# Attention on selected tokens: turning gathered rows by transposing DMA instead of on TensorE

## The chip, the cores and the metric

The kernel runs on one core of one Trainium2 chip. The metric is device time in microseconds (us) of one execution, from the slowest (here the only) core; less is better.

TensorE is called PE below (PEld is its weight load), VectorE DVE, ScalarE ACT, GpSimd POOL, and SyncE SP. SP computes nothing: it issues DMA transfers, in order, and waits before each until its source is ready. POOL here issues the indirect DMA transfers, which gather or scatter rows by a list of indices. Each engine runs its own instructions in order.

## The reference

Sixteen batches of x, each 512 features by 1024 tokens, get an attention layer with 8 heads of 64 features added. Query, key and value are the same projection. A token mask of zeros and ones decides which keys count, and rows of masked-out queries get uniform weights:

```python
xt = jnp.transpose(x, (0, 2, 1))
q = xt @ Wq.T
qh = q.reshape(B, T, NH, dk).transpose(0, 2, 1, 3)
scores = scale * jnp.einsum('bhqd,bhkd->bhqk', qh, qh)
logits = (scores * cmask + (1.0 - cmask) * NEG) * rmask
attn = jax.nn.softmax(logits, axis=-1)
ctx = jnp.einsum('bhqk,bhkd->bhqd', attn, qh)
out = ctx.transpose(0, 2, 1, 3).reshape(B, T, D) @ Wo.T
return x + jnp.transpose(out, (0, 2, 1))
```

## The kernel before, in words

**What is computed.** About half of the 1024 tokens of a batch are unmasked. The kernel packs them: per batch it computes on 544 columns (`C`), which hold the unmasked tokens first. A masked token's result is the projected mean of the values, so it needs only the mean of x over the tokens, kept as one more column (`CM`, column 544).

**Numbers.** Products that need float32 precision are made of float16 parts: a number a is split into a high part (a rounded to float16) and a low part (the remainder, in float16). A product takes three matmuls: high x high, low x high, high x low.

**The stages of a batch.**

- `slots` (for a group of batches) and `index` (L237 to L259, one batch) turn the mask into row numbers: eight small matmuls at L246 and an `idx` tile at L248; two masks of padding columns follow (L257, L259).
- `gather` (L319) posts five indirect transfers: four tiles `xa` of 128 tokens by 512 features in float32, and one tile `xt` of 32 tokens. `rows` (L310) issues them on POOL. The `xa` tiles are kept until the end of the batch's work, since the result is added to them and scattered back; they come from a ring of 13 buffers.
- `xt(b, k)` (L388) turns tile k, so that the features lie on the partitions. PE transposes it in blocks of 128 by 128 against an identity into a PSUM bank of the ring `pm` (L398; 16 large and 4 small blocks per batch). `xsplit` (L351) then splits the bank: ACT writes the high part into `xh` (L358), DVE the low part into `xl` (L359). After the fifth tile the mean column is added (L408, L355, L356).
- `query` (L411) multiplies `xh` and `xl` with the split weights, 12 matmuls for each of 8 combinations of a block of 128 features and a half of the columns (L421); ACT takes the result out of PSUM (L424). `qsplit` (L429) splits q on DVE, and four transfers on SP copy the parts into the tile `xx` (L442 to L445).
- `value` and `value_tail` transpose q for the values; `top` (L499) takes the largest squared length of q per head on DVE and turns it on PE (L509), and `bottom` (L513) makes the softmax shift of it.
- `scores` (L542) multiplies `xx` with itself (L580); ACT takes the exponential (L584). `attend` (L589) multiplies with the values (L597, L600).
- `recip_sums` and `recip_rows` (L608 to L642) take the inverse of the row sums. PE turns them (L633), DVE copies them out of PSUM (L636), SP writes them to DRAM (`rd<-rr`, L638) and reads them back spread over 64 partitions (`rb<-rd`, L641). `norm` (L645) multiplies with them on DVE (L664) and splits the result.
- `project` (L687) multiplies with the output weights (L680), DVE adds the result to the gathered tile (L685), POOL scatters it (L764). Masked tokens are gathered, added to and scattered by `late` and `rest` (L695 to L757).

**What sets the order.** `run` (L800 on) works on three batches at a time. While the scores of batch b go step by step (18 steps), a list `m` of other work is spread over the steps by the estimated cost of each entry: the last part of batch b-1 (its norm and projections), and the preparation of batch n = b+1 (`xt`, `query`, `value`). The list of a usual batch begins

```python
m = xt(n)[:1] + early[0] + xt(n)[1:2] + chunk2 + xt(n)[2:3] + early[1] + xt(n)[3:] + tp + query(n, 0, 0) + query(n, 0, 1) + bt + value(n, 0)
```

and the index and the gathers of batch b+2 come after the middle of it. A gather, a scatter or a `late` gather is not issued when it is posted: `issue` sends one transfer per step, and `once(dma, self.beat)` makes it wait for the latest matmul recorded at that time, so that POOL's transfers keep pace with PE. `later` puts a transfer of SP off to the next step. The tile framework then orders the instructions of each engine and sets the semaphores; `high_priority` moves an entry forward.

**Rings.** `pm` has two PSUM banks, which all small products share in turn: a bank is free again when its reader on ACT or DVE is done. The scores have two banks of their own (`pss`), so that PE can be two score tiles ahead of the exponentials.

Of the kernel before, what the change touches and what calls it, by code (L numbers as in the profile page):

```python
# [19 lines left out]
P = 128  # L20
# [14 lines left out]
CM = C  # L35
HG = H // 2
# [13 lines left out]
class Fast:  # L50
# [78 lines left out]
    def setup2(self):  # L129
# [4 lines left out]
        self.xh = fixed("xh", [P, DC, CQ], F16)  # L134
        self.xl = fixed("xl", [P, DC, CQ], F16)
        for t in (self.xh, self.xl):
            nc.gpsimd.memset(t[:, :, CM + 1:], 0.0)

# [10 lines left out]
    def load(self, name, c, half=None, after=None):  # L149
# [4 lines left out]
        raw = self.sb([P, D], F32, "xa", 13)[:, cols]  # L154
# [167 lines left out]
    def gather_now(self, b, j):  # L322
        s = self.st[b]
        if j < 4:
            s["xa"].append(self.rows(s["idx"][:, j:j + 1], self.sb([P, D], F32, "xa", 13)))
        else:
            s["xt"] = self.rows(s["idx"][:CT, 4:5], self.sb([P, D], F32, "xt"))
# [23 lines left out]
    def xsplit(self, dst, src, scaled=False):  # L351
        nc = self.nc
        with self.tc.high_priority(offset=HPO):
            if scaled:
                nc.vector.tensor_copy(self.xh[dst], src)  # L355
                self.xs = nc.vector.tensor_tensor(self.xl[dst], src, self.xh[dst], ALU.subtract).ins  # L356
            else:
                nc.scalar.activation(self.xh[dst], src, AF.Copy, scale=SX)  # L358
                self.xs = nc.vector.scalar_tensor_tensor(self.xl[dst], src, SX, self.xh[dst], ALU.mult, ALU.subtract).ins  # L359

    def range_x(self, b, c):
# [4 lines left out]
        nc.vector.tensor_reduce(s["top4"][:, c:c + 1], self.xh[:, c, :CM + 1], AX.X, ALU.max, apply_absolute_value=True)  # L366
# [21 lines left out]
    def xt(self, b, k):  # L388
# [3 lines left out]
        x = s["xa"][k] if k < 4 else s["xt"]  # L392
        if b == 0:
# [6 lines left out]
        self.xsplit((slice(None), slice(None), slice(k * P, k * P + n)), pt)  # L400
        self.last_xs = self.xs
        if k == 4:
            ms = self.sb([P, DC], F32, "ms", 2)
            m = s["ms2"].rearrange("p (c h) -> p c h", h=2)
            if b < 2:
                with self.behind(s["at"]):
                    nc.vector.tensor_tensor(ms, m[:, :, 0], m[:, :, 1], ALU.add)
            nc.vector.tensor_scalar(ms, ms if b < 2 else s["ms2"][:, :DC], SX / T, None, ALU.mult)  # L408
            self.xsplit((slice(None), slice(None), CM), ms, True)

    def query(self, b, e, g):  # L411
# [7 lines left out]
        for c in range(DC):  # L419
            for w, xx in ((wh, self.xh), (wh, self.xl), (wl, self.xh)):  # L420
# [74 lines left out]
    def shift(self, b, g):  # L495
# [639 lines left out]
```

## Time and profile before

| What | Value |
|---|---|
| Three timed runs | 1137.52, 1138.30, 1139.32 us; median 1138.3 |
| The profiled execution | 1133.56 us; span from its first to its last instruction 1131.8 us |
| Instructions | 23296 |
| Granted TensorE clock, mean | 0.992 of full speed |
| DMA | 181.35 MB in 78122 packets, mean 160 GB/s |
| HBM | 92.34 MB read, 33.91 MB written |

How to read the profile: the page gives the busy time of each engine as a share of the span, then the same in 40 equal slices of it, one digit per slice in tenths (9 is 90% or more). Then come the DMA queues with packets, MB and the share that their packets took of the time of 16 DMA engines (q1 is that of SP's transfers, q0 that of POOL's indirect ones). The chain is the work that ended last, followed back from the last instruction to what released each step. In a row of costs, the line number is that of the kernel, `out<-in` names the tiles, then come the partitions x elements of each and the number of instructions; behind the first bar stand the busy time in us and the mean length of one in ns, behind the second the idle time of that engine just before them, with what ended most of it. Matmuls overlap, so the length of one is more than its share of the busy time.

### The profile page before, as it was taken

The numbers are of one execution on the slowest core, as the hardware profiler recorded it, in microseconds if no ns is written. First come the engines' busy times: TensorE is split into PE (matmuls) and PEld (weight loads), VectorE is DVE, ScalarE is ACT, GpSimd is POOL, SyncE is SP. The second block draws the span as 40 slices with busy tenths as digits, with TensorE's granted clock in tenths as the row PEclk, the third lists the DMA queues.
The fourth block names the chain that finished last, engine by engine and source line by source line (L and its number), as shares of the span: only waits on it lengthen the run. The fifth ranks groups of instructions, "written<-read, shape, count | busy, mean of one in ns | idle before, by whom it ended". The sixth has DMA issues, their size and how long they took to land.

```text
span 1131.8 us, 23296 instructions
## 1 busy us (share of the span) xinstructions
PE 1090.5 (96%) x8386; PEld 707.9 (63%) x8386; DVE 731.6 (65%) x2369; ACT 676.2 (60%) x1716; POOL 289.1 (26%) x303
## 2 busy tenths in 40 slices
PE   7899999999999999999999999999999999998997
PEld 6566666666666666566666666566666666665543
DVE  6687567675665767667665666856576675655643
ACT  5776666666566666566565665666656566654540
POOL 3101021322202222222222232222222232214642
PEclk9899999999999999999999999999999999999999
DMA  6745554656546454655655566455655654545652
GB/s 212 218 117 151 143 159 128 191 142 179 149 127 175 124 201 137 171 175 158 189 150 165 154 177 185 129 181 144 195 166 156 188 152 130 149 126 174 204 161 77
DMA packets 78122, 181.35 MB, mean 160 GB/s; under 512 B 15008, under 2 KB 16800, under 8 KB 78000
## 3 DMA queue, kind: packets, MB, share of 16 engines
q1 hardware_dynamic: 56816, 111.62, 35.6%
q0 software_dynamic: 21184, 68.18, 18.7%
q8 instruction: 68, 1.11, 0.4%
q14 instruction: 54, 0.44, 0.1%
HBM read 92.34 MB, written 33.91 MB: 112 GB/s over the span
## 4 chain that ended last, share of the span: by engine, by line
PE 66%; DVE 14%; DMA 11%; issue 5%; ACT 2%; POOL 1%; SPq 1%; DVEq 0%; POOLq 0%; ACTq 0%
PE pav L597 19%; PE pss L580 16%; PE pm L680 13%; PE pm L421 8%; DMA rb<-rd 4%; PE pm L398 2%; DMA rd<-rr 2%; PE pav L600 2%; DMA xi<-x_in,idx 2%; PE pm L467 1%; DVE c L664 1%; DMA xx<-hl 1%; PE pm L633 1%; DVE tmp L458 1%; PE pss L555 1%
## 5 line engine op out<-in xcount | busy, mean ns | idle before, releaser
L584 ACT ACTIVATE p<-pss,nm 128x544 f32<-128x544 f32 x512 | 363.3, 714 | 231.5 <-PE pss L580 219.5
L580 PE MATMUL pss<-xx 128*128 128x272 f16 x2048 | 303.0, 281 | 4.2 <-DMA xx<-hl 2.7
L597 PE MATMUL pav<-p,v 128*64 128x272 f32 x2048 | 297.5, 402 | 0.9 <-ACT c L604 0.9
L580 PEld LDWEIGHTS <-xx 128*128 128x128 f16 x2048 | 192.1, 99 | 85.4 <-issue 41.2
L597 PEld LDWEIGHTS pav<-p,v 128*64 128x64 f32 x2048 | 140.6, 137 | 105.4 <-issue 40.9
L764 POOL DMA_INDIRECT y_out<-xa,idx x68 | 70.9, 1043 | 302.4 <-PE pss L580 163.6
L421 PE MATMUL pm<-xh,wqh 128*128 128x274 f16 (+1 forms) x512 | 143.9, 281 | 0.1
L421 PE MATMUL pm<-xl,wqh 128*128 128x274 f16 (+1 forms) x512 | 143.2, 280 | 0.2 <-DVE xl L359 0.2
L421 PE MATMUL pm<-xh,wql 128*128 128x274 f16 (+1 forms) x512 | 143.3, 280 | 0.0
L313 POOL DMA_INDIRECT xa<-x_in,idx x68 | 70.0, 1029 | 184.6 <-PE pss L580 89.3
L421 PEld LDWEIGHTS <-wqh 128*128 128x128 f16 x1024 | 99.9, 99 | 21.9 <-issue 3.4
L584 ACT ACTIVATION_READ_ACCUMULATOR p<-pss,nm 128x1 f32 x512 | 102.7, 201 | 0.0
L685 DVE SCALAR_TENSOR_TENSOR xa<-pm,xa 128x512 f32<-128x512 f32 x60 | 41.4, 689 | 89.6 <-PE pm L680 89.5
L313 POOL DMA_INDIRECT xi<-x_in,idx x60 | 59.6, 994 | 153.9 <-PE pss L555 53.9
L680 PE MATMUL pm<-woh,ch 128*128 128x512 f16 x240 | 91.0, 379 | 0.3 <-DVE ch L667 0.3
L680 PE MATMUL pm<-woh,cl 128*128 128x512 f16 x240 | 91.1, 379 | 0.1
L680 PE MATMUL pm<-wol,ch 128*128 128x512 f16 x240 | 91.0, 379 | 0.0
L424 ACT ACTIVATE q<-pm 128x272 f32<-128x272 f32 (+1 forms) x128 | 51.0, 398 | 64.0 <-PE pm L421 63.8
L764 POOL DMA_INDIRECT y_out<-xi,idx x60 | 60.9, 1015 | 92.0 <-PE pss L580 72.9
L664 DVE TENSOR_TENSOR c<-c,rb 128x544 f32<-128x544 f32 x64 | 46.2, 722 | 49.2 <-DMA rb<-rd 42.5
L680 PEld LDWEIGHTS <-ch 128*128 128x128 f16 x480 | 46.1, 98 | 41.0 <-DVE ch L667 0.8
L751 DVE TENSOR_TENSOR xi<-xi,ub 128x512 f32<-128x512 f32 (+1 forms) x60 | 40.1, 687 | 40.2 <-DMA xi<-x_in,idx 27.7
(191 smaller groups left out, 1585.5 us busy)
## 6 DMA issues: line engine op xcount, KB each, us to landing
xx<-hl SPq DMA_DIRECT2D x256, 136.0 KB
xm<-x_nat_in SPq DMA_DIRECT2D x56, 512.0 KB
rb<-rd SPq DMA_DIRECT2D x128, 136.0 KB
pt<-c SPq DMA_DIRECT2D x64, 136.0 KB
pt<-p SPq DMA_DIRECT2D x64, 136.0 KB
ub<-ud SPq DMA_DIRECT2D x16, 256.0 KB
xi<-x_nat_in SPq DMA_DIRECT2D x8, 256.0 KB
xa<-x_in,idx POOLq DMA_INDIRECT x68, 4.3
```

Of the source, the lines that this page charges most:

```text
L313: dma = self.nc.gpsimd.indirect_dma_start(out=tile[:n], out_offset=None, in_=self.x, in_offset=bass.IndirectOffsetOnAxis(ap=idx, axis=0))
L398: self.pe = nc.tensor.transpose(pt[:, c, :], x[:n, c * P:(c + 1) * P], self.ident[:n, :n]).ins
L421: self.beat = nc.tensor.matmul(pq, lhsT=w[:, c, e * P:(e + 1) * P], rhs=xx[:, c, cols], start=(k == 0), stop=(k == 3 * DC - 1)).ins
L424: nc.scalar.activation(s["q"][:, e, cols], pq, AF.Copy, scale=1.0 / (SX * SW))
L580: self.beat = nc.tensor.matmul(pt[:, g, :CH], lhsT=xx[:, 2 * k, i * P:(i + 1) * P], rhs=xx[:, 2 * k + a, g * CH:(g + 1) * CH], start=(a == ...
L584: self.exp = [nc.scalar.activation(t.rearrange("p (g c) -> p g c", g=2), pt[:, :, :CH], AF.Exp, bias=s["nm"][p // HG][:, p % HG:p % HG + 1 ...
L597: nc.tensor.matmul(s["pav"][k * DK:(k + 1) * DK, g, :CH], lhsT=s["v"][p][:, i, k * DK:(k + 1) * DK], rhs=ps[k][:, cols], start=(i == 0), s ...
L664: nc.vector.tensor_tensor(c, c, s["rb"][p], ALU.mult)
L680: nc.tensor.matmul(po[:cols.stop - cols.start], lhsT=a[:, e, cols], rhs=w[:, e, :], start=(e == 0 and k == 0), stop=(e == DC - 1 and k == 2))
L685: self.nc.vector.scalar_tensor_tensor(x, po, 1.0 / (SX * SW), x, ALU.mult, ALU.add)
L751: self.nc.vector.tensor_tensor(x[:n], x[:n], s["ub"][:n], ALU.add)
L764: dma = self.nc.gpsimd.indirect_dma_start(out=self.out, out_offset=bass.IndirectOffsetOnAxis(ap=idx, axis=0), in_=x, in_offset=None)
```

## The change

The transposes of batches 2 to 15 no longer run on PE. Batches 0 and 1 go as before. For the others, a new function `turn` splits a gathered tile where it lies, tokens on the partitions, into a float16 tile `hx` with the high and the low part side by side (128 x 1024). A transposing DMA transfer on SP then writes it, turned, into the tile `xhl`, which holds high and low part of all 8 blocks of features and has two buffers, since batch b+2 is now turned while batch b+1 is still read. Its rows are 560 wide (`CX`) instead of 546. The mean column is written twice (columns 544 and 545) in place of a mean and a zero.

The order moves too. The index of b+2 comes behind the first two queries of batch n instead of at the end of the list's middle part; its gathers are posted right after it; the five `turn` entries stand among the queries and values of the second half. `top` is cut in two: its DVE part (`peaks`) comes sooner than its transpose. The ring `xa` grows from 13 to 15 buffers, and the DMA descriptor scratch is set to 4096 bytes per partition; before, the kernel left it at its default.

```diff
+    def room(self, b):
+        s = self.st[b]
+        s["xhl"] = self.sb([P, 2 * DC, CX], F16, "xhl", 2)
+        s["xh"], s["xl"] = s["xhl"][:, :DC], s["xhl"][:, DC:]
+
+    def xsplit(self, hi, lo, src):
+        nc = self.nc
+        nc.scalar.activation(hi, src, AF.Copy, scale=SX)
+        self.xs = nc.vector.scalar_tensor_tensor(lo, src, SX, hi, ALU.mult, ALU.subtract).ins
+
+    def turn(self, b, k):
+        nc, s = self.nc, self.st[b]
+        n = P if k < 4 else CT
+        x = s["xa"][k] if k < 4 else s["xt"]
+        if "xhl" not in s:
+            self.room(b)
+        hx = self.sb([P, 2, D], F16, "hx", 2)
+        self.xsplit(hx[:n, 0], hx[:n, 1], x[:n])
+        out, src = s["xhl"][:, :, k * P:k * P + n], hx[:n].rearrange("p a d -> p (a d)")
+        self.later(lambda: nc.sync.dma_start_transpose(out=out, in_=src))
+        if k == 4:
+            self.mean(b)
...
-            s["xa"].append(self.rows(s["idx"][:, j:j + 1], self.sb([P, D], F32, "xa", 13)))
+            s["xa"].append(self.rows(s["idx"][:, j:j + 1], self.sb([P, D], F32, "xa", 15)))
...
-                m = xt(n)[:1] + early[0] + xt(n)[1:2] + chunk2 + xt(n)[2:3] + early[1] + xt(n)[3:] + tp + query(n, 0, 0) + query(n, 0, 1) + bt + value(n, 0)
-                m += query(n, 1, 0) + late + P_(0) + query(n, 1, 1) + P_(1)
+                ahead = b + 2 < B
+                index = [(0.5, L(self.index, b + 2))] if ahead else []
+                take = lambda *js: [(0, L(self.gather, b + 2, j)) for j in js] if ahead else []
+                turn = lambda k: [(0, L(self.turn, b + 2, k))] if ahead else []
+                m = early[0] + pk + (xt(n)[:3] if n == 1 else []) + chunk2 + (xt(n)[3:] if n == 1 else [])
+                m += query(n, 0, 0) + early[1] + tp + query(n, 0, 1) + bt + index + value(n, 0) + take(0, 1, 2, 4)
+                m += query(n, 1, 0) + late + P_(0) + take(3) + query(n, 1, 1) + P_(1)
                 m += [(0, L(self.range_x, n, c)) for c in range(DC)]
-                r = P_(2) + value(n, 1) + [(0.25, L(self.value_tail, n, 0))] + query(n, 2, 0) + query(n, 2, 1)
-                r += query(n, 3, 0) + [(0.1, L(self.top, n, 0))] + value(n, 2) + query(n, 3, 1)
-                r += [(0.1, L(self.bottom, n, 0))] + P_(3) + value(n, 3)
-                r += [(0.25, L(self.value_tail, n, 1)), (0, L(self.means, n))]
-                if b + 2 < B:
-                    m += [(0.5, L(self.index, b + 2))]
-                    r[1:1] = [(0, L(self.gather, b + 2, j)) for j in range(5)]
+                r = P_(2) + turn(0) + value(n, 1) + [(0.25, L(self.value_tail, n, 0))] + query(n, 2, 0)
+                r += [(0, L(self.peaks, n, 0))] + turn(1) + query(n, 2, 1)
+                r += [(0.1, L(self.top, n, 0))] + query(n, 3, 0) + turn(2) + value(n, 2) + query(n, 3, 1)
+                r += [(0.1, L(self.bottom, n, 0))] + turn(3) + P_(3) + value(n, 3)
+                r += [(0.25, L(self.value_tail, n, 1))] + turn(4) + [(0, L(self.means, n))]
...
-    nc = bacc.Bacc("TRN2", target_bir_lowering=False, num_devices=1)
+    nc = bacc.Bacc("TRN2", target_bir_lowering=False, num_devices=1, dynamic_dma_scratch_size=4096)
```

## The prediction

> **What bounds the kernel now.** I read the page's busy table and the 40 slices first, then one row for the middle of the run, then the costs by line with shapes kept apart, then the waits.
>
> ```profile
> span 1131.8 us, 23296 instructions
> PE 1090.5 (96%) x8386; PEld 707.9 (63%) x8386; DVE 731.6 (65%) x2369; ACT 676.2 (60%) x1716; POOL 289.1 (26%) x303
> PE   7899999999999999999999999999999999998997
> PEclk9899999999999999999999999999999999999999
> DMA  6745554656546454655655566455655654545652
> ...
> q1 hardware_dynamic: 56816, 111.62, 35.6%
> q0 software_dynamic: 21184, 68.18, 18.7%
> ...
> PE 66%; DVE 14%; DMA 11%; issue 5%; ACT 2%; POOL 1%; SPq 1%; DVEq 0%; POOLq 0%; ACTq 0%
> ```
>
> PE is full in all slices but the first and the last few, at full clock, and holds two thirds of the chain. The next row is the stretch from the first to the last of the steady-state transposes (us; then busy us of PE, PEld, DVE, ACT, POOL; clock, DMA share, GB/s).
>
> ```profile
> 49.30:984.40 935.10, 919.91 (x7143) 602.01 (x7144) 624.89 (x2032) 584.82 (x1480) 222.90 (x220) 1.00 0.55 159
> ```
>
> In 935 us PE idles 15.2 us, about 1.1 us in each of the 14 batches of some 67 us. DVE is at 67%, ACT at 63%, DMA at 55%. So PE bounds every batch: PE work taken out is time gained unless a new wait puts it back. The rows that go, or lie next to what is new:
>
> ```profile
> L398 PE MATMUL pm<-ident,xa 128*128 128x128 f32 x240 | 37.5, 280 | 2.1 <-DVE tmp L487 1.3 <-ACT v L469 0.5
> L398 PE MATMUL pm<-ident,xt 32*128 32x32 f32 x60 | 6.5, 227 | 0.0
> L359 DVE SCALAR_TENSOR_TENSOR xl<-pm,xh 128x512 f16<-128x512 f32 x60 | 39.9, 684 | 19.5 <-ACT xh L358 18.7
> L358 ACT ACTIVATE xh<-pm 128x512 f16<-128x512 f32 x60 | 34.8, 600 | 10.4 <-PE pm L398 9.9
> L163 DVE SCALAR_TENSOR_TENSOR wol<-xa,woh 128x512 f16<-128x512 f32 x4 | 2.7, 670 | 0.0
> L162 ACT ACTIVATE woh<-xa 128x512 f16<-128x512 f32 x4 | 2.4, 634 | 0.0
> ```
>
> 280 ns is the length of one transpose, but they are pipelined: 37.5 us over 240 is 0.156 us each, 6.5 over 60 is 0.108.
>
> **1. Transposes leave PE.** Batches 0 and 1 keep theirs; 14 batches lose 16 large and 4 small ones each: 224 x 0.156 + 56 x 0.108 = 41 us. In the PE timeline at 443 to 449 us one batch's run takes 1.02 + 0.59 + 0.50 + 0.36 = 2.47 us, times 14 = 35 us. I take **-38** (-41 to -35). The PE waits in front of them go too: 2.1 us in the first row, nothing in the second; **-2** (-4 to 0). What is late next is the exponentials and DVE's chain, costed in 3 and 4.
>
> **2. The split reads SBUF instead of PSUM.** Same number of ACT and DVE instructions. The weight split (L162, L163) does the same from SBUF: ACT 634 for 600 ns, DVE 670 for 684 ns; 56 times that is +1.9 us on ACT, -0.8 us on DVE, on engines with a third of their time free. **0**. It also moves: the copies and subtractions leave the crowded start of a batch for its second half. Into the start come the index (1.22 us of DVE at L242, 0.17 at L248) and the two pad masks (0.35 + 0.30), some 2.0 us, where 4 x 0.68 + 0.28 = 3.0 us of subtractions leave: **0**; if the cover fails, PE's eight small index matmuls (L246) wait up to 1.2 us per batch (+17).
>
> **3. A new wait on ACT.** In the changed program's order, in 12 of the 14 batches ACT's copy of the second gathered tile stands directly behind the exponential of the same scores that release that gather. Nearest rows: a gather into xa lands 2.7 / 3.7 / 8.3 us (min, median, max) after its issue. Let the scores end at 0. ACT does one or two exponentials (0.71 us each) and the first tile's copy (0.6), and is at the second copy by about 2; the rows land at 3.7; the copy ends at 4.3. Queued behind it are the next exponentials. PE has, after those scores, one projection (12 at 0.216 = 2.6 us), half an attend (1.0) and eight score matmuls (0.9); at 4.5 us it needs a score bank that an exponential from 4.3 to 5.0 frees. So PE waits 0.5 us; nothing if the rows land in 2.7; 1.8 us if they take 5.0, as the xi gather issued at 449.23 did. 12 x 0.5 = **+6** (0 to +22). The third tile's copy comes 4 us after its release, the tail's later still; the fourth's gather waits for a scatter (landing median 3.4), but ACT gets there at about the same time: 0.
>
> **4. Transposing transfers on SP's queue.** No row shows one. Each moves 256 KB; 70 are added (56 full, 14 of a quarter size), 59.5 full ones. By bytes: q1 moved 111.62 MB in 0.356 x 16 x 1131.8 us, 17.3 KB per engine-us, 277 GB/s on 16; 256 KB take 0.95 us. By packets: q1's cost 0.356 x 16 x 1131.8 / 56816 = 0.113 us each; if each 256-byte row of a 128-column block is a packet, 1024 of them on 16 engines take 7.2 us. I take 0.95, the nearest row being xx<-hl, SBUF to SBUF as well, whose 136 KB take SP 0.46 to 0.60 us to issue and land in 4.0 (493.71 us in the chain). Then DMA gains 57 us of work, 55% to 60%: harmless. What is queued behind on SP is the point. A transfer waits there for DVE's subtraction; behind it stand the four xx<-hl issues of a query, then rd<-rr, then rb<-rd, for which DVE's L664 waits already:
>
> ```profile
> L664 DVE TENSOR_TENSOR c<-c,rb 128x544 f32<-128x544 f32 x64 | 46.2, 722 | 49.2 <-DMA rb<-rd 42.5 <-SPq L1105 4.8 <-ACT p L584 1.9
> L685 DVE SCALAR_TENSOR_TENSOR xa<-pm,xa 128x512 f32<-128x512 f32 x60 | 41.4, 689 | 89.6 <-PE pm L680 89.5
> ```
>
> Behind L664 on DVE stands the next projection's L685, which frees one of the two pm banks, and the next rr copy, which frees the other. Before, rr at 468.25 led to rb at 476.73, 8.5 us, and PE hardly noticed. After, the third tile's subtraction (0.68) and its transfer (0.95) come ahead, so rb lands about 1.6 us later; PE, meeting both banks, pays about half: 14 x 0.8 = **+11** (0 to +28, if none or all of 2 us reaches PE). That queries wait for transfers I cost at nothing: tiles 0 to 3 are turned some 20 us before the query that reads them, and the first query waits for tiles 0 to 2 only. Cover lost, it is a landing, 4 us per batch.
>
> *A rule against the change.* PE's row shows 0.280 us for one block, 0.156 in a row. The Trainium skill, page "VectorE: DVE Perf Modes", section "The three transpose paths", gives 390 ns on TensorE and 1309 ns by DMA for a 128x128 block, and advises TensorE where PSUM will do as the target. Laid end to end, eight blocks would be 10.5 us per transfer (an estimate from that page), and the sum would be that of the slower rival below. The page "Advanced Engine Details and Errata", section "X-Bar Transpose (TRN2)", says that on trn2 such DMAs are as fast as regular ones, 350 to 400 GB/s, which makes 0.7 us (an estimate again) and the sum as here. No run here yet shows which.
>
> **5. The rest.** POOL issues the same gathers and scatters; those of batch b+2 go some 25 us sooner, onto a queue at 24%, and two more xa buffers (15) hold them. The smaller descriptor scratch has no row: from nothing to each of 284 indirect transfers waiting for the one before (3.7 us); POOL's instructions now take 0.9 to 1.0 us and mostly wait for PE, so **0**. Start and end keep their work: 0 (-3 to +3).
>
> **Sum:** -38 - 2 + 6 + 11 = -23 us. The profiled execution took 1133.56 us (span 1131.8 and 1.8 around it), so 1110.6 for it; the three timed runs have a median 4.7 us above that, and 1138.3 - 23 = **1115 us**.
>
> **Rivals.**
> - *The gain is kept almost whole.* For it: before, a 42.5 us wait of DVE for rb left PE at 98%; gathers may land under 3.7. Then -38 - 2 + 0 to 3: about 1099.
> - *Slower: the transfer is dear.* If one costs nearer 7.2 us than 0.95, SP is held, and the xx, rd and rb transfers of the same queue stand behind it; DMA goes to 55% + 59.5 x 7.2 / 1132 = 93%. rb then lands 7.9 us later instead of 1.6; with about 3 us taken up by slack PE waits 5 us per batch in place of 0.8: -40 + 6 + 70 = +36, some 1174. It decides from the point where PE loses 2.8 us per batch, at a transfer of about 5 us. Against it: only the count of packets speaks for it.
> - *The change does not do what it says:* transposes stay on PE or gathers are not sooner. The program's order shows 280 transposes gone and the index moved; hardly possible.
> - *A new bound:* ACT at 585 of 910 us and DVE at 625 of 910 stay under 70%. Not likely.
>
> **Chances.** Forecast (1103 to 1130): 0.46. Kept whole (under 1103): 0.23. Waits eat the gain but for a few us (1130 to 1136): 0.04; to within 0.2%, about what a measurement of this kernel can tell from no change: 0.05. Slower: 0.22, of which the dear transfer 0.14 and a sum of the upper bounds of 2, 3 and 4 (-40 + 17 + 22 + 28 = +27, 1165) 0.08. Faster is 0.46 + 0.23 + 0.04 = 0.73. The range goes from 1095, the fast end of the case kept whole, to 1145, which takes in the beginning of the slower one; outside are 0.04 below and 0.16 above.
>
> **What would show it.** Step 1: PE busy near 1050, and no L398 row after batch 1. Step 3: ACT's split copy with a wait for the xa gather of 1 to 2 us, a dozen times. Step 4: SP's transpose issues near 1 us each, and the wait of c for rb above 42.5 but PE idle under 2.5 us per batch; issues of 4 us or more, or DMA over 75%, would bring the slower case. PE waiting for an index, or for a transposed tile, would show steps 2 or 4 wrong.

## The result, and the profile after

| | Before | After |
|---|---|---|
| Median of four runs each | 1138.0 us (1137.5 to 1139.3) | 1194.4 us (1192.9 to 1199.6) |
| Profiled execution (span) | 1133.56 us (1131.8) | 1195.61 us (1193.9) |
| PE busy / idle in the span | 1090.5 / 41.3 us | 1081.8 / 112.1 us |
| Mean granted TensorE clock | 0.992 | 0.971 |

After over before is 1.050 (95% interval 1.047 to 1.053): slower, where 1115 us and a range of 1095 to 1145 had been predicted.

The page of the changed kernel, with the engines' busy time, PE and its clock in 40 slices, DMA, SP's and POOL's queues, and the chain that ended last:

```profile
span 1193.9 us, 22892 instructions
PE 1081.8 (91%) x8106; PEld 688.2 (58%) x8106; DVE 734.5 (62%) x2369; ACT 683.7 (57%) x1716; POOL 297.2 (25%) x301
PE   7899989898898999989799897998999899899997
PEclk9899999999899999999989999999999999999999
DMA  6746845757564584866648666474866648545552
...
q1 hardware_dynamic: 119984, 127.22, 42.3%
q0 software_dynamic: 21184, 68.18, 18.7%
...
PE 38%; DMA 20%; DVE 16%; issue 15%; ACT 4%; SPq 3%; POOL 3%; DVEq 0%; POOLq 0%; ACTq 0%
```

PE was full in all slices but the ends; now every third or so is an 8 or a 7. PE's share of the chain fell from 66% to 38%, and DMA, DVE and "issue" stand in it. DMA itself is far from full. Where PE stands idle, and who else waits, by the list of waits (us in total, times, the longest):

```profile
DVE c L696 <- DMA rb<-rd: 115.9, 30, 8.0
...
ACT hx L356 <- DMA xa<-x_in,idx: 59.5, 35, 3.1
...
PE pm L492 <- DVE m L540: 38.6, 13, 4.5
```

DVE's wait for `rb` went from 42.5 to 115.9 us. PE's largest wait is a new one: the transposes of q (L492) stand still for `m` (L540), a small DVE reduction that reads one of the two `pm` banks; 13 times, so once in nearly every batch.

**Bookkeeping.** The clock costs (1 - 0.971) x 1193.9 = 34.6 us after and (1 - 0.992) x 1131.8 = 9.1 before, so +25. PE's busy time fell by 8.7; without the clock it would be 34 less. PE's idle time rose by 70.8. So -34 + 25 + 71 = +62 us, which is the difference of the profiled executions. The work did leave PE; the waits and the slower clock took almost three times as much.

### The profile page after: what moved, and what is told of

The parts are those of the page before. It is cut to its first block, busy times and chain, and to the rows that moved or that the text cites. A ratio compares the mean times of both kernels' runs of the same rounds, so it can differ in the third digit from the quotient of the medians.

```text
span 1193.9 us, 22892 instructions
## 1 busy us (share of the span) xinstructions
PE 1081.8 (91%) x8106; PEld 688.2 (58%) x8106; DVE 734.5 (62%) x2369; ACT 683.7 (57%) x1716; POOL 297.2 (25%) x301
## 3 DMA queue, kind: packets, MB, share of 16 engines
q1 hardware_dynamic: 119984, 127.22, 42.3%
## 4 chain that ended last, share of the span: by engine, by line
PE 38%; DMA 20%; DVE 16%; issue 15%; ACT 4%; SPq 3%; POOL 3%; DVEq 0%; POOLq 0%; ACTq 0%
PE pav L626 10%; PE pss L609 9%; DMA xa<-x_in,idx 7%; PE pm L712 6%; PE pm L446 6%; DMA rb<-rd 6%; DMA rd<-rr 3%; DMA xi<-x_in,idx 2%; ACT p L613 2%; POOL y_out L796 2%; PE pm L492 2%; PE pav L629 1%; DVE c L696 1%; DVE hl L461 1%; DVE cl L700 1%
## 5 line engine op out<-in xcount | busy, mean ns | idle before, releaser
L609 PE MATMUL pss<-xx 128*128 128x272 f16 x2048 | 312.1, 286 | 18.1 <-ACT p L613 14.1
L609 PEld LDWEIGHTS <-xx 128*128 128x128 f16 x2048 | 196.6, 101 | 102.4 <-issue 56.0
L446 PE MATMUL pm<-xhl,wqh 128*128 128x272 f16 (+1 forms) x1024 | 190.5, 283 | 1.9 <-ACT q L449 0.8
L446 PE MATMUL pm<-xhl,wql 128*128 128x274 f16 (+1 forms) x512 | 144.8, 283 | 0.0
L696 DVE TENSOR_TENSOR c<-c,rb 128x544 f32<-128x544 f32 x64 | 46.2, 722 | 126.2 <-DMA rb<-rd 115.9
L310 POOL DMA_INDIRECT xi<-x_in,idx x60 | 66.6, 1111 | 115.4 <-PE pss L609 52.7
L717 DVE SCALAR_TENSOR_TENSOR xa<-pm,xa 128x512 f32<-128x512 f32 x60 | 41.2, 687 | 72.9 <-PE pm L712 68.6
L356 ACT ACTIVATE hx<-xa 128x512 f16<-128x512 f32 x56 | 35.2, 629 | 85.1 <-DMA xa<-x_in,idx 59.5
L492 PE MATMUL pm<-ident,q 128*128 128x128 f32 x256 | 44.9, 297 | 41.0 <-DVE m L540 38.6
L494 ACT COPY v<-pm 128x512 f32<-128x512 f32 x64 | 37.5, 585 | 74.4 <-PE pm L492 72.7
```

What stands on the lines that cost most here:

```text
L310: dma = self.nc.gpsimd.indirect_dma_start(out=tile[:n], out_offset=None, in_=self.x, in_offset=bass.IndirectOffsetOnAxis(ap=idx, axis=0))
L446: self.beat = nc.tensor.matmul(pq, lhsT=w[:, c, e * P:(e + 1) * P], rhs=xx[:, c, cols], start=(k == 0), stop=(k == 3 * DC - 1)).ins
L492: nc.tensor.transpose(pv[:, k, :], s["q"][:, e, k * P:(k + 1) * P], self.ident)
L494: nc.scalar.copy(v, pv)
L609: self.beat = nc.tensor.matmul(pt[:, g, :CH], lhsT=xx[:, 2 * k, i * P:(i + 1) * P], rhs=xx[:, 2 * k + a, g * CH:(g + 1) * CH], start=(a == ...
L696: nc.vector.tensor_tensor(c, c, s["rb"][p], ALU.mult)
```

## One stall, read through the trace

Three engines in one window from the middle of the changed kernel. SP first (start, length, operation):

```profile
566.28 1.24 SPq L369 DMA_TRANSPOSE xhl<-hx  x1
567.97 0.47 SPq L467 DMA_DIRECT2D xx<-hl  x1
568.55 0.53 SPq L468 DMA_DIRECT2D xx<-hl  x1
569.14 0.58 SPq L469 DMA_DIRECT2D xx<-hl  x1
569.77 0.59 SPq L470 DMA_DIRECT2D xx<-hl  x1
570.40 0.52 SPq L667 DMA_DIRECT2D rd<-rr  x1
574.22 1.10 SPq L670 DMA_DIRECT2D rb<-rd  x2
...
580.09 3.37 SPq L369 DMA_TRANSPOSE xhl<-hx  x2
583.55 0.47 SPq L667 DMA_DIRECT2D rd<-rr  x1
586.47 1.11 SPq L670 DMA_DIRECT2D rb<-rd  x2
```

DVE in the same window (in brackets: idle before, and for whom):

```profile
566.17 0.27 DVE L665 COPY rr<-pm 10x128 f32<-10x128 f32 x1
...
577.84 0.73 DVE L696 TENSOR_TENSOR c<-c,rb 128x544 f32<-128x544 f32 x1 [7.72 <-DMA rb<-rd]
578.48 0.68 DVE L717 SCALAR_TENSOR_TENSOR xa<-pm,xa 128x512 f32<-128x512 f32 x1
...
581.74 0.27 DVE L665 COPY rr<-pm 10x128 f32<-10x128 f32 x1
...
590.42 0.73 DVE L696 TENSOR_TENSOR c<-c,rb 128x544 f32<-128x544 f32 x1 [3.60 <-DMA rb<-rd]
...
594.27 0.28 DVE L540 TENSOR_REDUCE m<-pm 128x1 f32<-128x128 f32 x1
```

And PE:

```profile
579.22 0.33 PE L662 MATMUL pm<-ident,rcol 128*128 128x128 f32 x1 [1.70 <-DVE xa L717]
...
588.71 0.33 PE L538 MATMUL pm<-ident,smcol 128*128 128x128 f32 x1
...
594.61 0.66 PE L492 MATMUL pm<-ident,q 128*128 128x128 f32 x4 [3.25 <-DVE m L540]
```

The row sums `rr` of the first pair of heads are ready at 566.44. SP is busy with a transposing transfer and has four `xx` in its order before `rd`, which goes at 570.40, 4.0 us late; in before the median was 0.44. (Below, "late" is the median over all 16 batches. It is 3.7 to 4.9 us in nine of them; in batches 0, 2, 5, 8, 11, 14 and 15 the first pair's `rd` goes at once.) DVE reaches c at 570.1, and stands there for 7.7 us. Behind c is the read of a `pm` bank (L717), so PE's next small product waits: 1.70 us. For the second pair two transposing transfers, 3.37 us together, stand ahead of `rd`. DVE stops at c again (3.60 us), and now has a whole split of q behind c and ahead of `m`. PE wrote the bank that `m` reads at 588.71; it gets it back at 594.55.

Not every stall at L492 runs like this. In batches 2, 5, 8 and 11 the second pair's c waits only 0 to 1.6 us for `rb`, and PE still stands for 2.5 to 3.1 us: DVE had stopped 0.8 to 1.9 us for gathered rows (`xi`) just ahead, and then does c and eleven other operations before `m`.

Then the clock. Stretches from the start of the span, in us; the columns are busy us of PE, PEld, DVE, ACT, POOL, then granted clock, DMA share and GB/s:

```profile
586.00:594.00 8.00, 5.36 (x55) 3.41 (x53) 4.34 (x13) 3.99 (x10) 2.27 (x3) 1.00 0.53 197
594.00:597.00 3.00, 1.81 (x10) 0.97 (x10) 2.83 (x14) 1.33 (x3) 0.00 (x0) 0.85 0.83 189
597.00:603.00 6.00, 5.72 (x27) 3.85 (x29) 4.62 (x14) 1.61 (x4) 0.92 (x1) 0.51 0.53 130
603.00:610.00 7.00, 7.00 (x48) 4.12 (x46) 2.91 (x12) 3.20 (x9) 0.10 (x1) 1.00 0.47 119
```

After the stall PE runs at half clock for some 7 us: 3.4 us lost on top of the 3.25.

## The experiments

**Theory.** The transposing transfers hold SP, `rd` goes late, c stands on DVE in front of the readers of both `pm` banks, PE stops, the clock drops. **Rivals:** the new order of the entries is what costs (`peaks` and `top` above all, or the earlier gathers); ACT's waits for gathers and the two `hx` buffers; the DMA load; the descriptor scratch. Ratios are to before on the same chip.

### Is it the order of `top`?

```diff
-                r += [(0, L(self.peaks, n, 0))] + turn(1) + query(n, 2, 1)
-                r += [(0.1, L(self.top, n, 0))] + query(n, 3, 0) + turn(2) + value(n, 2) + query(n, 3, 1)
+                r += turn(1) + query(n, 2, 1) + query(n, 3, 0)
+                r += [(0, L(self.peaks, n, 0)), (0.1, L(self.top, n, 0))] + turn(2) + value(n, 2) + query(n, 3, 1)
```

> The changed kernel in which only the order of one place goes back: the transpose of the largest square (`top`) of batch b+1 comes behind both queries of block 3 again, as before the change, and its DVE part directly ahead of it. In the changed kernel's profile PE waits 38.6 us (13 times) at L492 for DVE's m (L540), which frees a bank of pm, and DVE is late there because m stands behind c<-rb (L696). Theory A (the transposing transfers hold up SP's queue, so that rd<-rr is issued 3.7 us late for the first pair of heads and 1.5 us for the second, DVE is late, and whichever reader of a pm bank comes next holds PE): m is no longer what PE waits for, but L717, rr and q take its place; at most a third comes back: 1175 to 1195 us, and the wait of c for rb stays above 90 us. Rival B (the sooner place of the transpose is the cause): the 38.6 us go and with them most of the clock steps that follow such waits (13 to 16 steps of 1.7 us): 1130 to 1150 us.

1194.7 us, 1.052 (1.047 to 1.057). PE's wait for `m` at L492 is gone, and L662 waits instead (39 us for `m` and `rcol`); c still waits 106 us. The product that meets the held bank changed, not the loss.

### Is it the `hx` ring?

```diff
-        hx = self.sb([P, 2, D], F16, "hx", 2)
+        hx = self.sb([P, 2, D], F16, "hx", 3)
```

Paid for with one `xa` buffer less (14):

> The changed kernel with three hx buffers in place of two; to make room, the ring of xa has 14 buffers instead of 15. In the changed kernel's profile ACT reaches the copy of the third tile while the transposing transfer of the first still runs (5.9 to 6.8 us from issue to the copy that waits for it), and stands there for 1 to 3.9 us; the exponentials, the copies of q and the next transposing transfer on SP queue behind it. Theory C (the two buffers make ACT wait for a landing, and that is the start of SP's delay): the wait of hx for xhl goes, rd<-rr of the first pair is issued 1 to 2 us after rr instead of 3.7, and 10 to 30 us come back: 1165 to 1185 us. Rival A (the transfers' own issue time and place on SP): the delay of rd stays, 1188 to 1200 us. If 14 buffers of xa are too few, gathers start later and ACT's wait for xa grows from 59.5 us.

1197.5 us, 1.054 (1.048 to 1.060), a miss, but a telling one. `rd` goes at once (0.03 us for both pairs) and c waits only 18.8 us. The time went elsewhere: ACT's wait for gathers doubled, and holds the exponentials that PE needs.

```profile
ACT hx L356 <- DMA xa<-x_in,idx: 121.6, 48, 5.9
...
PE pss L609 <- ACT p L588: 35.3, 13, 4.9
```

So with 14 `xa` buffers the gathers come late (with 15, next, ACT waits 70.8 us for them), and this rival can take the time without a late `rd`. Paid for with half the scratch instead:

> The changed kernel with three hx buffers, and xa left at its 15; the room comes from the DMA descriptor scratch, 2048 bytes instead of 4096. With 14 xa buffers the third hx buffer took away the delay of rd (3.7 us to 0.03 for the first pair) and most of c's wait for rb (115.9 to 18.8 us), but ACT waited 121.6 us for xa instead of 59.5, and PE 50 us for p. Theory C (the landing of the transposing transfer, met through two hx buffers, is what delays SP, DVE and PE; the 14 buffers were a second wait of their own): ACT's wait for xa is back near 60 us, c's wait for rb below 40, the clock's loss under 20 us, and the time 1135 to 1165 us. Rival D (the copies that wait for gathers hold PE through p, whatever the buffers): ACT's wait for xa stays above 100 us and the time above 1180 us.

1183.8 us, 1.045 (1.040 to 1.050). ACT's wait for the transposing transfer went from 10.1 to 0.6 us, `rd` is as late as before (3.67 and 1.45) and c waits 111 us. The ring is worth some 1% at the most.

### The transfers away

The turned tile of two batches ago is read instead, and the transposing transfers are left out:

```diff
-        self.later(lambda: nc.sync.dma_start_transpose(out=out, in_=src))
```

> The changed kernel without the 70 transposing transfers: ACT and DVE still split every gathered tile into hx, but nothing carries it to xhl, and batches 2 to 15 compute on the turned columns of batches 0 and 1 (that part of the computation is left out). All other places stay, the sooner top and the sooner gathers too. Theories A and C together (everything lost comes through the transfers: SP's queue and the wait for a landing): rd<-rr follows rr by less than 0.5 us in the median of each pair, c waits for rb under 45 us, PE idles under 2.5 us per batch, and the time is that of the forecast's first terms, 1095 to 1115 us. Rival B (the place of top) or D (ACT waiting for gathers that come late): c's wait falls, but PE still waits for m or for p, and the time stays above 1140 us.

1125.1 us, 0.990 (0.986 to 0.994): 69 us from the transfers alone. `rd` goes at once, c waits 34.3 us, the clock is back at 0.991. The early order, with the tiles turned by PE:

> The changed kernel with the transposes put back on PE, at the place that they have in the order for batch 1, so no turn, no hx and no transposing transfer; index and gathers half a batch sooner, peaks ahead of top, the smaller descriptor scratch and the two xhl buffers stay. It is the rest of the change without its main part. Theories A and C: the rest costs little, 1132 to 1150 us, and DVE's wait for rb is near the 42.5 us of before. Rivals B and D (order and gathers cost by themselves): 1160 us or more.

1151.5 us, 1.014 (1.010 to 1.018), unexpectedly above before. PE's turns stand in it where batch 1 has them, so it isn't the change's order alone. With the gathers put back to their old place:

> As the run with the transposes on PE and early gathers (1151.5 us), with the index and the gathers back at their places of before; peaks and top keep their new places. If the early index and gathers cost the 15 us, 1134 to 1142 us; if the order of queries, peaks and top does, 1146 to 1154 us.

1164.4 us, 1.024 (1.017 to 1.030): the earlier gathers help there, by about 1%, and do not cost. What costs in this order stays open.

The spans of these profiles make a chain: before 1131.8; early order +11.6 (1143.4); no turning on PE -21.6 (1121.8), made of PE busy 1096.9 - 1055.6 = -41 and idle 46.5 to 66.2 = +20; transfers +72.1 (1193.9).

### Is it the length of the transfers?

The four large turns as plain transfers of the same bytes:

```diff
-        self.later(lambda: nc.sync.dma_start_transpose(out=out, in_=src))
+        if k < 4:
+            flat = hx.rearrange("p a (c t) -> p (a c) t", t=P)
+            self.later(lambda: nc.sync.dma_start(out=out, in_=flat))
+        else:
+            self.later(lambda: nc.sync.dma_start_transpose(out=out, in_=src))
```

> The changed kernel in which the four large transfers of a batch are plain ones, with the same source, target, size and 256-byte rows, so that the parts reach xhl unturned (the turning of those tiles is left out; the fifth, small tile is turned as in the changed kernel). Theory C1 (it is the transposing that makes the landing slow): a plain transfer lands in about 4 us like xx<-hl, so ACT does not wait for hx, SP's issue falls from 1.26 to about 0.5 us, and the time is near the run without transfers, 1120 to 1140 us. Rival C2 (the bytes in rows of 256, or the place on SP's queue, are dear however they are moved): 1170 us or more, with the wait of hx for xhl still there.

1144.6 us, 1.007 (1.005 to 1.009). An issue takes 0.64 us in place of 1.26, `rd` of the first pair is late by 3.2 to 4.1 us in eight batches and goes at once in the other eight, that of the second goes at once (0.03 in the median), c waits 36.7. But DVE's order came out different as well, with c behind the read of the bank for the first pair in most batches, so that this run doesn't tell the two apart.

### Moving transfers and turns

Turns later among the queries (`value(n, 1)`, its tail, `turn(0)`, and so on; the others likewise behind the entry that they preceded):

> The changed kernel with each of the first four turns one place later in the order (behind the value or query that it stood ahead of); nothing else moves. Theory D (ACT stands waiting for gathered rows, 59.5 us in 35 copies, and PE then for p): that wait falls under 25 us and 15 us or more come back, to 1165 to 1180 us. Rival C (the wait for the landing of the first transfer is what counts): the copies keep their distances, the third still waits for hx, and the time stays at 1188 to 1200 us.

1188.5 us, 1.050 (1.043 to 1.056). ACT's wait for gathers is 58.4 us (59.5 in the changed kernel), c waits 113. This with the old order of `top` and three `hx` buffers:

> Three hx buffers (scratch 2048 bytes), the turns one place later, and top behind both queries of block 3 again, all in one. If the waits for the landing, for the gathers and for m are all that the transfers cost, the time comes to that of the run without transfers (1125 us) or below, 1105 to 1130 us, and beats the kernel before. If SP's queue or the DMA engines cost by themselves, it stays above 1140 us.

1188.6 us, 1.048 (1.045 to 1.051); c waits 111. Neither touches what costs. Then `rd` ahead on SP:

```diff
-        nc.sync.dma_start(out=rd, in_=rr)
+        with self.tc.high_priority(offset=HPO):
+            nc.sync.dma_start(out=rd, in_=rr)
```

> The changed kernel with one priority added: the write of the row sums, rd<-rr, goes ahead of the four xx<-hl of the query in SP's order, as it does in the run without transposing transfers and in the kernel before; in the changed kernel, with the same source, the order is transposing transfer, xx four times, rd. The transposing transfers themselves keep their places ahead of it. Theory A (the order on SP that the transposing transfers bring about is the cause): the delay of rd for the pair behind the first three turns falls from 3.7 us to about 1.3, c's wait for rb from 115.9 to some 80 us, and 15 to 25 us come back: 1165 to 1180 us. Rival (SP's order is only one symptom, PE waits for something else): 1188 us or more.

1175.5 us, 1.032 (1.027 to 1.038). `rd` is late by 0.81 and 1.79 us, since the transposing transfers still stand ahead of it; c waits 75.8. And with the third tile's transposing transfer also put behind `rb`, through `self.behind(self.rb)`:

> As the run that sets only rd ahead of xx, and besides the third tile's transposing transfer is ordered behind the rb transfers of that pair, so that none of the large transfers stands between rr and rd there (the fourth stands ahead of the next pair's rd, with its 1.26 us). Theory A: rd follows rr at once for the first of the two pairs, within 1.4 us for the next; c's wait for rb is below 55 us, PE's waits for m, rcol and xa are those of the run without transfers, the clock's loss below 18 us, and the time 1130 to 1155 us. Rival C (the landing of 6 to 9 us through two hx buffers): the third transfer now starts later, the fifth copy waits for it, and the time stays above 1170 us.

1163.5 us, 1.022 (1.020 to 1.025). `rd` at once (0.03 and 0.05), c waits 53.2 us, PE waits for `m` 25.8 still. ACT pays for the delayed transfer at the `hx` ring (28.9 us). The steps 1194, 1175, 1163 follow c's wait, 116, 76, 53 us, but a prompt `rd` alone does not bring back 1125. Of PE's waits for `m` that are left, 17 of 25.8 us come in batches 2, 5, 8 and 11, where the second pair's c waits 0.1 us or less for `rb`, and DVE stands 1.6 to 5.7 us ahead of it, at the operation on gathered rows (`xi`).

Gathers back in the second half, all turns at the end of the list:

```diff
+                r += query(n, 3, 0) + [(0, L(self.peaks, n, 0)), (0.1, L(self.top, n, 0))] + value(n, 2) + turn(0) + query(n, 3, 1)
+                r += [(0.1, L(self.bottom, n, 0))] + turn(1) + P_(3) + turn(2) + value(n, 3) + turn(3)
...
+                r[1:1] = take(0, 1, 2, 3, 4)
```

> The changed kernel with the order of before (index at the end of the middle part, gathers from the start of the second half, top behind both queries of block 3), and the five turns spread over the last third of the list, so that their transposing transfers come around the row sums of the last pair, early in the next batch, and none of them ahead of the two pairs that were late. Theory A: rd follows rr at once for those two pairs; about 0.2 to 0.5 us per batch is lost on the last pair instead; ACT's wait for gathered rows is under 20 us; and since the order of before comes back too (worth up to 15 us by the run with early gathers and the transposes on PE), the time is 1105 to 1130 us. Against it: the first queries of the next batch read tiles 3 and 4 some 10 us after their transfers are issued; if they land later, PE waits for q, and the time is 1150 us or more.

1143.7 us, 1.006 (1.004 to 1.008). c waits 25.5 us. Now PE waits for turned tiles, 14.5 us in 7 stalls of up to 2.7, and at a mean clock of 0.972 over the profiled span of 1148.6 us the clock costs 32 us, against 9 in before (the other four executions had 0.978 to 0.981). Two attempts at a place between, with three `hx` buffers and the transfers and `rd` ahead on SP:

> A version made from the findings: the order of before, with the index one projection and the gathers one entry sooner than before; the five turns spread from query 3 to the end of the list; three hx buffers (scratch 2048); rd ahead of xx on SP; the transposing transfers with a priority of their own, so that they are on their way before the next batch's queries. Theory A: rd is on time, c waits under 45 us for rb, no query waits for xhl (14.5 us in the run with the turns at the end) and the time is 1105 to 1130 us, under both kernels. If the landing or the copies still bite, 1135 us or more.

1161.5 us, 1.019 (1.015 to 1.024).

> As the other version, with the index one query and the gathers one step sooner and the first two turns behind top: the gathers have more time to land, so that ACT waits less for rows. If ACT's wait for rows still holds PE through p, this is 3 to 10 us faster than the other; if the place of the early gathers costs (as in the run with the transposes on PE), it is slower by as much.

1157.9 us, 1.018 (1.013 to 1.022). The first missed what was expected. The second was to be 3 to 10 us faster than the first if ACT waited less for rows; it is 3.7 us faster, which the two intervals do not tell from nothing, and ACT's wait is the same (50.6 and 50.8 us). c waits 65 and 68 us, and PE stands at L665 for `rcol` 23 and 26 us.

### The scratch

Before, with `dynamic_dma_scratch_size=4096`:

> The kernel before with one thing of the change: 4096 bytes of DMA descriptor scratch per partition in place of the default. The run with early gathers and the transposes on PE took 1151.5 us against 1136.2 of before, and this takes one part out of that. If the scratch is the reason, 1145 to 1152 us, with gathers or scatters that land later; if the order is the reason, as before, 1133 to 1140 us.

1135.3 against 1137.0 us, 0.999 (0.998 to 1.001): no effect.

### A late `rd` without transposing transfers

To the kernel without transfers, four writes of `rr` to a tile that nobody reads are added ahead of `rd` for the first two pairs:

```diff
+        for _ in range({0: 4, 1: 4}.get(p, 0)):
+            nc.sync.dma_start(out=self.dram.tile([10, P], F32, tag="rx", name="rx"), in_=rr)
```

> The run without transposing transfers, with a delay put in by hand: four small extra writes of the row sums (5 KB each, to DRAM that nothing reads) stand ahead of the real rd<-rr of the first two pairs of heads of every batch. In some batches the four xx transfers come between them, as in the changed kernel. As in the run without the transfers, batches 2 to 15 compute on the columns of batches 0 and 1. No transposing transfer is there, so no long landing, no wait for hx. Theory A (a late rd is enough by itself): rd is 2 to 4 us late for the first pair and 1.5 us for the second, c waits 80 to 120 us for rb, PE waits for m (L538 there) and rcol again, the clock steps come back, and the time rises from 1125 to 1150 to 1175 us. Rival (the transposing transfers cost through the DMA engines or their landings): it stays within 10 us of 1125.

1127.0 us, 0.990 (0.987 to 0.994). `rd` was late by 4.56 and 1.47 us, about as late as after the change or later, and the time stayed within 2 us of no_transfer: c waits 28.5 us, and PE's transposes of q, here L490, no longer wait for `m`:

```profile
L490 PE MATMUL pm<-ident,q 128*128 128x128 f32 x256 | 42.9, 283 | 8.4 <-DVE q L450 6.2 <-ACT q L447 1.7 <-DVE idx L245 0.3
```

The theory as I had stated it fell. The reason stands in DVE's order: in this kernel c comes behind the read of the bank in the first pair and behind most of the split of q in the second (`m` is still behind c there, but c comes late enough to wait only 0 to 1.9 us for `rb` in batches 1 to 14). So the theory needs both: a late `rd` **and** c ahead of the banks' readers.

### c later, SP untouched

The whole change stays, transfers and all. Only c's multiplication of the first two pairs is put behind the split of q, `m` and the last projection's read on DVE, and its step in the list one later:

```diff
-        nc.vector.tensor_tensor(c, c, s["rb"][p], ALU.mult)
+        with self.behind(*((self.split_last, self.max_last, getattr(self, "plus_last", self.max_last)) if p < 2 and b < self.B - 1 else ())):
+            nc.vector.tensor_tensor(c, c, s["rb"][p], ALU.mult)
...
-                            free.setdefault(st + 5, []).append(L(self.norm, b, p))
+                            free.setdefault(st + (6 if p < 2 and b < B - 1 else 5), []).append(L(self.norm, b, p))
```

> The changed kernel with nothing moved on SP: the transposing transfers stand ahead of rd as in the changed kernel. Only DVE's order differs: the first operation of the norm of the first two pairs, c<-c,rb, is ordered behind the work that stood right behind it, the projection's xa<-pm,xa for the first pair and the query's split and m<-pm for the second, as it came to stand in the run with the late writes and no transposing transfers (rd_slow, 1127 us, where rd was 4.6 and 1.5 us late and c waited 12.5 and 7.5 us for rb). Theory A2 (rd is late through the transposing transfers, and it costs because DVE's order, fixed beforehand, has c too early and the readers of the pm banks behind it): rd stays about 3.7 and 1.5 us late, c's wait for rb falls from 115.9 below 60 us, PE's wait for m goes, and the time is 1130 to 1160 us. Rival (the transposing transfers' own load or landing): 1175 us or more, with PE waiting for other readers.

1135.2 us, 0.997 (0.9945 to 0.9997): 59 us of the loss gone. Its page and its two rows:

```profile
span 1131.8 us, 22906 instructions
PE 1060.2 (94%) x8106; PEld 677.7 (60%) x8106; DVE 733.9 (65%) x2369; ACT 679.9 (60%) x1716; POOL 306.9 (27%) x301
```

```profile
L697 DVE TENSOR_TENSOR c<-c,rb 128x544 f32<-128x544 f32 x64 | 46.2, 721 | 32.1 <-DMA rb<-rd 26.6 <-SPq L1141 5.4
L492 PE MATMUL pm<-ident,q 128*128 128x128 f32 x256 | 41.8, 282 | 7.2 <-DVE m L540 4.4 <-ACT q L449 1.4 <-DVE q L452 0.8
```

And the same place of the same batch, SP and then DVE:

```profile
541.87 1.24 SPq L369 DMA_TRANSPOSE xhl<-hx  x1
...
545.99 0.53 SPq L667 DMA_DIRECT2D rd<-rr  x1
549.76 1.10 SPq L670 DMA_DIRECT2D rb<-rd  x2
...
551.60 4.62 SPq L369 DMA_TRANSPOSE xhl<-hx  x2
556.46 0.32 SPq L667 DMA_DIRECT2D rd<-rr  x1
```

```profile
541.76 0.27 DVE L665 COPY rr<-pm 10x128 f32<-10x128 f32 x1
...
550.54 0.68 DVE L718 SCALAR_TENSOR_TENSOR xa<-pm,xa 128x512 f32<-128x512 f32 x1
553.45 0.73 DVE L697 TENSOR_TENSOR c<-c,rb 128x544 f32<-128x544 f32 x1 [2.22 <-DMA rb<-rd]
```

For the first pair SP does what it did at 566.28 to 575.3 above, to within 0.05 us, and `rd` is as late. But DVE frees the bank (L718) first and reaches c when `rb` is nearly there: 2.22 us where it stood 7.72. ACT's waits are about those of the changed kernel, 62.6 us for gathers and 8.5 for transposing transfers (59.5 and 10.1 there), so that these rivals do not explain the loss.

For the second pair `rd` is no longer late (0.03 us in the median, 1.48 in the changed kernel), though nothing was moved on SP: the split of the next gathered tile (L357) no longer stands behind c, so its transfer starts earlier (9.7 us behind that of the first pair in this batch, 13.8 before), and both are done when `rr` comes. So c's place held up that transfer too, and this run does not keep the lateness of both pairs. rd_slow does, at 1127 us (1.47 us in its second pair), but without the transfers.

The first pair of heads, by run:

| | `rd` in time | `rd` late |
|---|---|---|
| c ahead of the next read of a bank (`xa<-pm,xa`) | no_transfer, 1125 us (0.03 us late) | after, 1194 us (3.72) |
| c behind it | not run | c_later, 1135 us (3.94); rd_slow, without transfers, 1127 us (4.56) |

Last, this with `rd` ahead on SP and three `hx` buffers:

> DVE's order as in that run, rd ahead of xx on SP, and three hx buffers (scratch 2048): the three cures that each gave something by themselves, without moving turns, queries or gathers. If they add, the time comes near that of the run without transposing transfers, 1120 to 1140 us; if the landing and the gathers' waits on ACT are what is left, 1140 to 1160 us.

1131.3 us, 0.9925 (0.990 to 0.995), a little below the kernel before. What is left of the transfers' cost is 10 us in the spans of c_later and no_transfer (1131.8 and 1121.8).

## Why the prediction was wrong, step by step

- **Step 1, transposes leave PE: right.** -38 predicted (-41 to -35); -34 in the bookkeeping, just outside, and -41 between early_pe and no_transfer.
- **Step 2, split and index: split right, order open.** ACT's copy took 629 ns and DVE's subtraction 692. No PE wait for an index shows among the largest; but early_pe is 11.6 us of span above before, of which the step had nothing.
- **Step 3, ACT's wait for gathers: mechanism right, size too small.** 35 waits of up to 3.1 us were seen where a dozen of 1 to 2 were named. PE waits 14.1 + 1.6 us for exponentials, against +6 (0 to +22); in no_transfer, where nothing of step 4 is left, 12.4 us against 1.6 in early_pe. "The third tile's copy ... 0" missed the ring: two `hx` buffers, each kept until its transfer landed, made ACT wait 10.1 us more.
- **Step 4 is what failed**: "rb lands about 1.6 us later; PE, meeting both banks, pays about half: 14 x 0.8 = +11 (0 to +28, if none or all of 2 us reaches PE)". The term of +11 came to some 62 us, of the 72 that the transfers cost in all. The price of a transfer was near: 0.95 us taken, 1.26 measured at SP. From `rr` to c it became 2.7 us longer in the first pair (8.19 to 10.87) and 2.6 in the second (5.67 to 8.30), in two pairs of a batch where I counted one. The error is in "pays about half". I had named the readers behind c (the projection's read, the next `rr`), but took PE's patience from before, where c waited 42.5 us at little harm. In the second pair c stands ahead of the split of q and `m` as well, so PE pays the wait and that work. Late by 2.7 us in the median, c and the work around it cost a stall of up to 4.5 us in 13 of the 16 batches at L492, 38.6 us together, 10.9 more at L662 for L717 and 8.9 at L509 for `rr`. (In batches 2, 5, 8 and 11, 10.6 of the 38.6 us, c itself hardly waited; no_transfer, with the same order, has stalls of 1.3 to 2.4 us there.) c_later shows it: with that order changed and the transfers as they are, 62 of the transfers' 72 us of span are gone.
- **The clock was in no step.** In the changed kernel stalls of 2.3 us and more, all but one, were followed by half clock, 1.71 us lost in each stretch. The clock is +25 of the +62 us by which the kernel became slower.
- **Scratch, DMA load: 0, right.** The scratch was measured alone. The page's q1 and q0 went from 54.3% to 61.0% of 16 engines, and c_later carries the same transfers in 1135 us.
- **The rivals.** The slower one (0.14, 1174 us) named the place, SP held and `rb` late, but asked for a transfer of 5 us or more. 1.26 us was enough, since the point of decision was worked out with PE losing under half of the delay. "Kept whole", 1099, is not reached even without transfers: no_transfer stays at 1125, since its order stands 11.6 us of span above before (early_pe), and taking 41 us of work from PE brought 20 us of new idle time: 10.8 of it for exponentials (12.4 us against 1.6 in early_pe) and 4.9 for `m` (8.1 against 3.2).

*The rules weighed.* A transposing transfer took 1.26 us of SP, and the five copies that waited for one started 4.1 to 6.8 us after its issue. Its load on the DMA engines: q1 went from 35.4% x 16 x 1121.8 (no_transfer) to 42.3% x 16 x 1193.9 engine-us, 1726 more for 59.5 full transfers, 29 each, or 1.8 us on 16 engines. The Trainium skill's estimates were 10.5 us ("VectorE: DVE Perf Modes", "The three transpose paths", block by block) and 0.7 us ("Advanced Engine Details and Errata", "X-Bar Transpose (TRN2)"); SP's 1.26 us and the engines' 1.8 lie near the second, the 4.1 to 6.8 us to landing between the two, and neither decided the result.

What is argued and not shown: that the framework put c early because it took the transposing transfer for short. What is shown is that c's place decides whether the transfers cost 72 us or 10. The transfers did not move c: no_transfer has it at nearly the same place. No run has a late `rd` with c ahead and no transposing transfers, and what costs 11.6 us in early_pe's order stays open.

## What to carry to other kernels

Price a longer queue by what stands **behind** the waiting instruction on its in-order engine, up to the next reader of a shared bank, and not by the wait's own length: 2.7 us at c became a stall in nearly every batch and a slower clock. After such a change look first at the consumer's order; to let DVE do what is ready before it waits gave back 59 us, while the four that shifted single turns or added a buffer (hx_three, hx_room, late_turn, best1) gave 11 or less, `rd` ahead on SP 19, and 31 with one turn behind `rb`; all turns at the end, with the old order, gave 51. And add to a PE stall of 2 us and more what the halved clock may cost after it, here 1.7 us or twice that.

## What the runs showed of the hardware

- A transposing transfer of 256 KB takes 1.26 us to issue on SP, a plain one of the same size 0.64. In the changed kernel two back to back took 2.6 to 3.4 us.
- The granted clock falls to 0.5 for 3.4 us at a time. In the changed kernel 14 such stretches follow the first 150 us and come before the last 90, each in the wake of a PE stall of 2.3 to 4.5 us (two of the stalls had two), while one stall of 3.25 us (at 522 us) and three of 2.0 to 2.2 had none; c_later had one such stretch between these times. In turn_end three stalls of 1.97 to 2.06 us had one each (at 383, 591 and 879 us), so the length of a stall alone does not tell. The Trainium skill, "TensorE: Matmul & The Clock Gate", section "HAM oscillation — how this bites in real kernels", gives gaps of over about 3.4 us as the rule; here stalls from 1.97 us on were enough several times, and 3.25 us once were not.
- A late transfer costs next to nothing where its consumer comes late too: `rd` 4.56 us late in rd_slow left the time at 1127 us, against 1125 in no_transfer.
